# Two graph layers on one core: layer 1's constants and first load written beside layer 0, and the steps of a slot in another order

## The chip, the cores and the metric

The kernel runs on one core of one Trainium2 chip. The metric is device time in microseconds (us), as the median of several executions. The engines are TensorE (PE: matmuls; its weight loads, PEld, overlap them), VectorE (DVE), ScalarE (ACT), GpSimd (POOL) and SyncE (SP), which here only issues DMAs. Each engine takes its own instructions strictly in the order in which the program lists them, so an instruction that waits holds all that stands behind it on that engine.

## The reference

Sixteen graphs of 1024 nodes with 256 features go through two graph attention layers; each adds its result to its input and normalises the rows. Cut to what is computed:

```python
# layer 0: one head, dense softmax, three batch norms
Wh = einsum('bnf,of->bno', h, W);  ei = Wh @ a1;  ej = Wh @ a2
att = bn(ei[:, :, None] + ej[:, None, :], g1, b1)     # statistics over batch and rows
att = bn(where(att >= 0, att, 0.2 * att), g2, b2)
att = softmax(att, axis=2) * adj
x = layernorm(x + elu(bn(einsum('bij,bjo->bio', att, Wh), g3, b3)))

# layer 1: four heads, softmax over the neighbours only, mixed with softmax(adj)
fts = inputs @ Wh;  f1 = fts @ w1h + b1h;  f2 = fts @ w2h + b2h
logits = f1[:, :, None] + f2[:, None, :]
coefs = ah * softmax(leaky_relu(logits, 0.2) - 1e9 * (1 - adj)) + (1 - ah) * softmax(adj)
out = mean over heads of elu(coefs @ fts + bh + inputs)
x = layernorm(x + out)
```

The adjacency is sparse: a few neighbours in a thousand for most nodes, far more for the first ones.

## The kernel before

**Layer 0** (lines 200 to 645) is laid out by a scheduler that follows the dependencies and keeps each engine's list in an order near that of the code. It has three stages. *Projections* (lines 218 to 305): for each graph x is loaded (SP), transposed (PE), copied (ACT, L285), multiplied by WX (PE, L289) into one of four PSUM buffers `pw`, copied to `wx` (DVE, L293) and stored. The layer 1 weights W1s are loaded here too, and `WW` (the weights times w1 and w2) is made from them by DVE; `parameters1` loads bias, b1, b2 and alpha and waits for them on DVE. *Moments* (lines 318 to 512): statistics of the batch norms. *Aggregation* (lines 517 to 645): for each graph, weights (ACT, DVE), matmuls with `wh` (PE, L572), and a store to `h_dram` (SP, L599); `store` also collects sums, from which s3 and t3, scale and shift of the last batch norm, follow after the last graph.

**Between the layers.** Line 1023 makes t31. Then the pools of layer 1 open and lines 1035 to 1136 make its constants, nearly all on DVE: `IW` (identity and WW side by side), `MX` (mixes the heads), `bits`, `ibits`, `every`, `add16` (matmul weights that pack the bits of the adjacency into words), `cols`, `in8`, `in16`, `far`, `rows`, `low`, `act`, `lanes` (used to turn positions into lists of neighbours), the subtraction of W's last row `wl` from W1s, and the fixed parts of `fw` and `xr`. `wl` takes one of the two buffers that the rows of the adjacency (`rw`) and the lists' `B` use; `jj` one of those of `pi`. The pool `hpool` holds one buffer for a graph's h.

**Layer 1** (from line 1138) is written under `manual_schedule`: the order of the code is the order on each engine. For each graph g there is

- *Lists*: load_rows (SP, rw), words (PE: pc) and worded (ACT, DVE), used (DVE), places (PE: pp) and placed (DVE: hi, low), low and high (DVE: B, hA), higher (DVE), pick (PE: po, 64 matmuls) and picked (DVE), order (PE: pl) and indices (DVE: ix).
- *Graph*: load_h, exps (ACT) and elu (DVE), load_x, turn (PE: pz) and residual (DVE) and beside (ACT: fs) for eight blocks of rows, means, squares, spans, norm, factors, raised (ACT), scale (ACT, eight times 256 columns, L1481), table (SP: the scaled rows and their factors to `xe_dram`), spread, total (PE: pX) and store_total (SP: xr), gather_last and gathered (PE: pul, DVE: zl, ACT: sl), turn_last (PE: ptl).
- *Chunk*: fetch (POOL: an indirect DMA of neighbours' rows from `xe_dram` to xc) and weigh (DVE, one cast on ACT).
- *Unit*: sixteen per graph, two (hp 0 and 1) for each block of 128 rows: gather (PE: pu), invert (DVE: z), norm (ACT: s), turn (PE: pt) and turned (ACT: sT), linear (PE: pv), add (DVE: v), exps (ACT: m), sum, mean, squares, span, power (POOL), close (ACT), store (SP).

The PSUM pools are small: `ps_s` has two buffers, shared by pc, pz, pp, po, pl, pX, pA, pul and ptl; `ps_t` has one (pt), `ps_v` two (pv), `ps_u` three (pu).

The loop at line 1808 goes through slots n. In a slot, the unit n gathers, the unit n - 3 is turned, the unit n - 5 goes through linear, and so on, as the offsets in the code say. The side steps of the graphs (Lists, Graph, Chunk) stand in the slots that the tables `AT`, `FETCH` and `WEIGH` name, counted from the graph's first unit; a graph's steps begin 30 slots ahead of its first unit, so those of the next graph lie beside the units of this one, 16 slots apart. `side` sorts them into four lists for each slot: `early` (part 0: what reads a matmul's result, one slot after it), `first` (part 1: matmuls), `after` (part 2: DMAs and ACT), `late` (part 3: weigh). `gather(0)` has work only where hp is 0 (even slots: blocks 0 and 1), `gather(1)` in every slot. Slots of negative n, which have no units yet, are the lead of layer 1.

## Time and profile before

| | us |
|---|---|
| median of 3 runs | 2375.66 (2374.55 to 2377.97) |
| the profiled execution, as timed | 2380.35 |
| its span in the profile | 2378.5 |

| engine | busy us | share | instructions |
|---|---|---|---|
| PE | 2121.5 | 89% | 12631 |
| PEld | 1641.9 | 69% | 12631 |
| DVE | 1890.4 | 79% | 4624 |
| ACT | 1442.5 | 61% | 3172 |
| POOL | 1031.7 | 43% | 1133 |

How to read it. A group or timeline line names the engine, the line of the program (L1434), the operation, the tiles (what is written, an arrow, what is read) and the shapes; a number in brackets is the time for which the engine stood idle before it, and what ended that. The shares are averages over stages with different limits, so what a change is worth is read from its own stage: the moments keep DVE busy (80 of 115 us from 185 to 300), the aggregation PE, and in layer 1 both are busy most of the time. The granted clock of PE is 0.92 of full speed on average; it is low where PE's work is thin. A wait costs time only where the waiting engine, or one that waits for it, decides the end.

### The profile page before, as it was taken

To read this page: it belongs to the slowest core of one execution; us is meant where nothing else is said; L and a number is where in the kernel's file an instruction comes from. 1 tells how busy PE (TensorE), PEld (TensorE's weight loads), DVE (VectorE), ACT (ScalarE), POOL (GpSimd) and SP (SyncE) were. 2 spreads that over 40 slices of the span, in tenths; PEclk is the share of its full clock that TensorE was granted. 3 is DMA by queue.
4 is the path that set the end of the run, shared out by engine and by line. 5 is a ranking of instruction groups with operands and counts; after the bars stand their busy time and mean duration, and the time that the engine had idled before them with its cause. 6 is when DMAs were issued, how large, how long until landed. Compare 5 with 4: busy or idle time off the path is not lost. (4 is left out here: it accounts for less than half of the span.)

```text
span 2378.5 us, 37080 instructions
## 1 busy us (share of the span) xinstructions
PE 2121.5 (89%) x12631; PEld 1641.9 (69%) x12631; DVE 1890.4 (79%) x4624; ACT 1442.5 (61%) x3172; POOL 1031.7 (43%) x1133
## 2 busy tenths in 40 slices
PE   6992489999999549999999999999999999999997
PEld 5772434444444338878888788788888788887886
DVE  3335899999999446988888879888888889788786
ACT  1122777777776235567566665675776666757665
POOL 0000100000000037665766666756767666667682
PEclk9995589999999758999999999999999999999999
DMA  9969949986553258566575676675766756756551
GB/s 258 283 193 235 262 112 241 229 206 155 154 156 86 107 151 215 172 168 170 169 194 170 156 209 167 162 192 164 187 174 172 194 162 163 214 161 163 136 146 50
DMA packets 342358, 419.75 MB, mean 176 GB/s; under 512 B 172760, under 2 KB 273168, under 8 KB 336016
## 3 DMA queue, kind: packets, MB, share of 16 engines
q1 hardware_dynamic: 285840, 256.24, 36.7%
q0 software_dynamic: 55104, 158.54, 29.9%
q8 instruction: 102, 1.67, 0.3%
q10 hardware_dynamic: 1216, 2.51, 0.3%
q14 instruction: 96, 0.79, 0.1%
HBM read 346.47 MB, written 104.29 MB: 190 GB/s over the span
## 5 line engine op out<-in xcount | busy, mean ns | idle before, releaser
L1338 POOL DMA_INDIRECT xc<-xe_dram,ix x640 | 673.3, 1052 | 182.5 <-issue 162.0
L1635 PE MATMUL pv<-W1s,sT 128*128 128x256 f32 x2048 | 493.1, 384 | 0.3 <-ACT sT L1629 0.3
L572 PE MATMUL pa<-em,wh 128*128 128x512 f32 x1024 | 451.5, 599 | 18.0 <-DVE em L536 13.7
L1635 PEld LDWEIGHTS pv<-W1s,sT 128*128 128x128 f32 x2048 | 372.0, 192 | 40.9 <-ACT sT L1629 0.7
L572 PEld LDWEIGHTS pa<-em,wh 128*128 128x128 f32 x1024 | 193.6, 192 | 251.1 <-issue 236.4
L1543 PE MATMUL pu<-xc,w 128*125 128x256 f32 x1280 | 366.2, 408 | 0.0
L1615 PEld LDWEIGHTS pt<-MX,s 125*128 125x128 f32 x2560 | 338.2, 198 | 23.9 <-ACT sT L1625 6.3
L1615 PE MATMUL pt<-MX,s 125*128 125x100 f32 x2560 | 333.0, 279 | 4.4 <-ACT sT L1625 4.4
L1609 ACT ACTIVATE s<-pu,z 125x256 f32<-125x256 f32 x640 | 261.9, 477 | 21.6 <-DVE z L1601 21.4
L1543 PEld LDWEIGHTS pu<-xc,w 128*125 128x125 f32 x1280 | 243.5, 201 | 41.1 <-DVE v L1659 5.7
L1625 ACT COPY sT<-pt 128x500 f32<-128x500 f32 x256 | 148.5, 580 | 129.9 <-PE pt L1615 129.9
L1649 ACT ACTIVATE m<-v,neg 128x512 f32<-128x512 f32 x256 | 184.2, 719 | 49.9 <-DVE v L1643 37.0
L528 ACT ACTIVATE e<-eb,c,s 128x1024 f32<-128x1024 f32 x128 | 155.0, 1236 | 79.0 <-DVE sm L542 42.6
L1643 DVE TENSOR_TENSOR v<-pv,x 128x512 f32<-128x512 f32 x256 | 175.2, 684 | 12.4 <-PE pv L1635 12.0
L1451 ACT COPY fs<-pz 128x16 f32<-128x16 f32 x128 | 21.9, 171 | 250.9 <-DVE mv L1444 250.9
L532 ACT ACTIVATE e<-e,v,u 128x1024 f32<-128x1024 f32 x128 | 152.3, 1229 | 22.7 <-DVE e L531 16.6
L536 DVE TENSOR_TENSOR em<-e,mt 128x1024 f32<-128x1024 f32 x128 | 155.7, 1218 | 3.4 <-PE pa L572 2.1
L1434 PE MATMUL pz<-IW,h 128*128 128x136 f32 x512 | 94.0, 316 | 70.1 <-ACT fs L1451 27.1
L531 DVE SCALAR_TENSOR_TENSOR e<-e 128x1024 f32<-128x1024 f32 x128 | 151.5, 1217 | 0.0
L1434 PEld LDWEIGHTS pz<-IW,h 128*128 128x128 f32 x512 | 76.8, 208 | 90.6 <-ACT fs L1451 36.2
L147 POOL TENSOR_TENSOR s<-var,mhalf 128x2 f32<-128x2 f32 x1 | 0.7, 710 | 311.9 <-DVE var L146 311.9
L289 PE MATMUL pw<-WX,xT 128*128 128x266 f32 x512 | 124.5, 396 | 11.4 <-ACT xT L285 9.1
(319 smaller groups left out, 3602.2 us busy)
## 6 DMA issues: line engine op xcount, KB each, us to landing
x<-in_x_dram SPq DMA_DIRECT2D x32, 1024.0 KB
adj<-in_adj_dram POOLq DMA_DIRECT2D x16, 2048.0 KB, 16.7
rw<-adj SPq DMA_DIRECT2D x32, 1024.0 KB
A<-u_dram SPq DMA_DIRECT2D x128, 250.0 KB
wh_dram<-wx SPq DMA_DIRECT2D x16, 1024.0 KB
wh<-wh_dram SPq DMA_DIRECT2D x16, 1024.0 KB
h_dram<-hb SPq DMA_DIRECT2D x16, 1024.0 KB
h<-h_dram SPq DMA_DIRECT2D x16, 1024.0 KB
```

The costliest lines, as they stand in the source:

```text
L528: nc.scalar.activation(e, ebs[b], AF.Identity, bias=c1[:, k, b : b + 1], scale=s1[:, k : k + 1])
L532: nc.scalar.activation(e, e, AF.Exp, bias=v2[:, k : k + 1], scale=u2[:, k : k + 1])
L536: nc.vector.tensor_tensor(em, e, mts[b][:, k, :], ALU.mult)
L572: nc.tensor.matmul(acc[b, hf, oc], wh[b][:, k, oc * P : (oc + 1) * P], ems[b, k][:, hf * HALF : (hf + 1) * HALF], start=(k == 0), stop=(k ...
L1338: nc.gpsimd.indirect_dma_start(out=self.xc[:, i, :], out_offset=None, in_=xe_dram[g.b % 2], in_offset=bass.IndirectOffsetOnAxis(ap=g.l.ix[ ...
L1434: nc.tensor.matmul(pz[:, oc, :], self.h[:, oc, k * P : (k + 1) * P], IW[:, oc, :], start=True, stop=True,)
L1543: nc.tensor.matmul(pu[0:QR, 0:F], c.w[:, k].rearrange("p h q -> p (h q)"), c.xc[:, k, 0:F], start=(i == 0), stop=(i == len(OF[q]) - 1),)
L1609: nc.scalar.mul(f.s[0:QR, i], f.pu[i][0:QR, 0:F], f.z[0:QR, i : i + 1])
L1615: nc.tensor.matmul(self.pt[:, i].rearrange("p h q -> p (h q)"), self.first.s[0:QR, i, self.hp * P : (self.hp + 1) * P], MX[0:QR].rearrange ...
L1635: nc.tensor.matmul(self.pv[:, hh, :], self.first.sT[:, fc, self.hp * HP + hh, :], W1s[:, fc, self.hp * HP + hh, :], start=(fc == 0), stop= ...
L1643: nc.vector.tensor_tensor(self.v2, self.pv, self.g.x[:, self.it].unsqueeze(1).to_broadcast([P, HP, F]), ALU.add)
L1649: nc.scalar.activation(self.m, self.v2, AF.Exp, bias=neg1, scale=1.0)
```

## The change

The diff does three things.

1. The block that makes layer 1's constants moves, unchanged in what it computes, from between the layers to just behind the projections of layer 0. Its tiles get a pool of their own, `ek`, which is opened, together with `hpool`, ahead of layer 0 and closed at the end. `jj` and `wl` take the buffer of `hpool` (tag h) instead of those of `pi` and `rw`. In the list of the changed program the pieces lie on DVE among the copies of `wx` of the first five graphs, the iota on POOL at the very start, and `wl`'s DMA on SP behind the load of x of graph 9.
2. h of graph 0 is loaded to that buffer by a DMA written at n = 4 of the last graph of layer 0 (on SP it stands right behind the store of graph 0's h); `load_h` of graph 0 only takes it.
3. In layer 1 the order of the steps in a slot changes, and some entries of AT and FETCH move by one to three slots. On ACT, DVE and SP the steps of a slot keep their order relative to each other; on POOL, power stands at the head of the slot; on PE, gather(0) stands ahead of the side matmuls (`first`) instead of behind them.

```diff
+    m1 = ExitStack()
+    ek = m1.enter_context(tc.tile_pool(name="ek", bufs=1))
+    hpool = m1.enter_context(tc.tile_pool(name="hpool", bufs=1))

     with ExitStack() as l0:
...
             mts = {b: mask(mpool, b, "mt0") for b in range(min(2, B))}
+
+        TW = P + 2 * H
+        IW = ek.tile([P, C, TW], F32, name="IW")
+        for oc in range(C):
+            nc.vector.tensor_copy(IW[:, oc, 0:P], ident)
+        nc.vector.tensor_copy(IW[:, :, P:TW], WW)
...
+        jj = hpool.tile([P, K, NQ], I32, tag="h", name="jj")
+        nc.gpsimd.iota(jj, pattern=[[P, K], [0, NQ]], base=-N, channel_multiplier=1)
...
+        wl = hpool.tile([P, H, F], F32, tag="h", name="wl")
+        nc.sync.dma_start(wl, W[:, F - 1, :].partition_broadcast(P))
+        for fc in range(C):
+            nc.vector.tensor_tensor(W1s[:, fc], W1s[:, fc], wl, ALU.subtract)
+        nc.sync.dma_start(W1s[P - 1 : P, C - 1], bias1[0:1])
...
+        h0 = hpool.tile([P, C, N], F32, tag="h", name="h_0")

         epool = l0.enter_context(tc.tile_pool(name="epool", bufs=1))
...
+                    if n == 4 and b == B - 1:
+                        nc.sync.dma_start(h0, h_dram[0])
...
     with ExitStack() as l1:
         xpool = l1.enter_context(tc.tile_pool(name="x1pool", bufs=3))
-        hpool = l1.enter_context(tc.tile_pool(name="hpool", bufs=1))
         pk = l1.enter_context(tc.tile_pool(name="pk", bufs=1))
...
-        TW = P + 2 * H
-        IW = pk.tile([P, C, TW], F32, name="IW")
...
-        jj = pk.tile([P, K, NQ], I32, tag="pi", name="jj", bufs=1)
...
-        wl = pk.tile([P, H, F], F32, tag="rw", name="wl", bufs=2)
...
             def load_h(self):
                 b = self.b
+                if b == 0:
+                    self.h = h0
+                    return
...
         EARLY = 30
         AT = {
-            'lh': -29, ('rw', 0): -29, ('rw', 1): -28, ('words', 0): -24, ('words', 1):
-            -22, 'used': -20, 'places': -20, 'low': (-18, -18, -17, -15), 'high': (-19,
-            -15), 'higher': -14, 'pick': -14, 'order': -12, 'lx': -23, 'spans': -12,
-            'norm': -11, 'scale': (-11, -10), 'table': -9, 'spread': -10, 'total': -9,
+            'lh': -29, ('rw', 0): -29, ('rw', 1): -28, ('words', 0): -27, ('words', 1):
+            -22, 'used': -20, 'places': -20, 'low': (-18, -18, -17, -16), 'high': (-19,
+            -15), 'higher': -14, 'pick': -14, 'order': -11, 'lx': -23, 'spans': -12,
+            'norm': -11, 'scale': (-11, -11), 'table': -9, 'spread': -10, 'total': -9,
             'mean': (-17, -14), 'elu': (-26, -25, -24, -23), 'turn': (-22, -21, -19,
-            -19, -18, -17, -15, -15), 'gather': -4, 'turn last': -2,
+            -19, -18, -17, -15, -15), 'gather': -4, 'turn last': 0,
         }
 
         FETCH = {
-            'l': (-7,), 0: (-7, -7, -6, -6, -6), 'm': (-6, -6, -5, -5, -4), 'n': (-4,
-            -4), 1: (-4, -3, -3, -3, -2), 'o': (-2, -2), 2: (-1, -1, 0, 0, 0), 3: (1, 1,
-            1, 2, 2), 4: (2, 3, 3, 3, 3), 5: (3, 3, 4, 5, 5), 6: (5, 5, 6, 6, 7), 7: (7,
+            'l': (-7,), 0: (-7, -6, -6, -6, -6), 'm': (-6, -6, -5, -5, -4), 'n': (-4,
+            -4), 1: (-4, -3, -3, -3, -3), 'o': (-2, -2), 2: (-1, -1, 0, 0, 0), 3: (1, 1,
+            1, 1, 2), 4: (2, 3, 3, 3, 3), 5: (3, 4, 4, 4, 5), 6: (5, 5, 6, 6, 7), 7: (7,
             8, 8, 8, 10),
         }
...
             for n in range(-EARLY, len(units) + 12):
+                do(n - 9, "power")
                 do(n - 6, "add")
                 stand(0, n)
                 do(n - 6, "exps")
                 do(n - 3, "turn", "turned")
                 do(n - 1, "invert")
                 do(n - 1, "norm")
+                stand(2, n)
+                do(n - 10, "close")
+                do(n - 11, "store")
                 do(n - 5, "linear")
-                do(n - 9, "power")
-                stand(2, n)
+                if 0 <= n < len(units):
+                    units[n].gather(0)
                 stand(1, n)
-                do(n - 10, "close")
+                if 0 <= n < len(units):
+                    units[n].gather(1)
                 do(n - 7, "mean")
                 do(n - 8, "span")
                 stand(3, n)
-                do(n - 11, "store")
-                if 0 <= n < len(units):
-                    units[n].gather(0)
+                do(n - 6, "sum")
                 do(n - 7, "squares")
-                do(n - 6, "sum")
-                if 0 <= n < len(units):
-                    units[n].gather(1)
+    m1.close()
```

## The prediction

> **What bounds the kernel now.** I read the page first (span, busy shares, the 40 slices), then busy times by stage, then the waits of TensorE (PE), VectorE (DVE) and GpSimd (POOL) inside layer 1, then the timelines of the joint between the layers and of one graph.
>
> First two of the page's slices lines (busy tenths, 2378.5 us in 40), then the windows of three stages (length, busy us of PE, PE's weight loads, DVE, ACT, POOL, then granted clock, DMA share, GB/s): layer 0's aggregation, the joint, layer 1's loop.
>
> ```profile
> PE   6992489999999549999999999999999999999997
> DVE  3335899999999446988888879888888889788786
> ...
> 300.00:797.00 497.00, 488.17 (x1407) 237.67 (x1407) 455.73 (x534) 354.63 (x406) 8.11 (x12) 0.98 0.65 163
> 797.00:914.00 117.00, 56.63 (x407) 43.18 (x406) 65.77 (x278) 35.71 (x99) 38.61 (x37) 0.59 0.50 152
> 914.00:2357.00 1443.00, 1374.98 (x8969) 1193.23 (x8968) 1209.25 (x3340) 949.63 (x2529) 958.96 (x1032) 0.95 0.65 171
> ```
>
> Layer 0's aggregation is PE's (488 of 497 us). The joint, 797 to 914, is nobody's: PE works 57 of 117 us. Layer 1 looks like PE's (1375 of 1443), but the next two windows, of one graph, show two halves: 41 us in which PE never stops, then 46 us in which DVE is busy 44.83.
>
> ```profile
> 1662.00:1703.00 41.00, 41.00 (x299) 34.98 (x299) 31.38 (x83) 32.34 (x78) 25.24 (x28) 1.00 0.81 217
> 1703.00:1749.00 46.00, 42.74 (x254) 37.06 (x253) 44.83 (x134) 26.93 (x80) 34.38 (x37) 0.94 0.54 150
> ```
>
> PE's waits in layer 1 (in total, times, longest) all stand in that second half; DVE's long ones are for DMA, just ahead of it:
>
> ```profile
> PE pz L1434 <- ACT sl L1556: 23.3, 14, 1.7
> PE pz L1434 <- ACT fs L1451: 18.4, 12, 2.6
> PE pz L1434 <- DVE hi L1200: 13.8, 10, 2.3
> PE po L1259 <- ACT fs L1451: 6.1, 12, 0.5
> ```
>
> ```profile
> DVE mi L1353 <- DMA xc<-xe_dram,ix: 20.1, 8, 4.8
> DVE x L1444 <- DMA x<-in_x_dram: 17.2, 10, 2.8
> ```
>
> In the joint, the DVE timeline shows the constants ahead of the first ELU, and the first residual add waiting for x:
>
> ```profile
> 803.35 0.64 DVE L1038 COPY IW<-ident 128x128 f32<-128x128 f32 x2
> ...
> 812.63 1.27 DVE L1428 SCALAR_TENSOR_TENSOR h<-hm,h 128x512 f32<-128x512 f32 x2
> ...
> 822.85 0.42 DVE L1444 CUSTOM_DVE_ANT_0 x<-pz,x 128x256 f32<-128x256 f32 x1 [2.23 <-DMA x<-in_x_dram]
> ```
>
> And PE, in one graph (pz waits; matmuls after a wait; the pick group po):
>
> ```profile
> 1653.17 6.03 PE L1259 MATMUL po<-hA,B 128*128 128x64 f16 x64 [0.50 <-ACT fs L1451]
> ...
> 1716.04 0.76 PE L1434 MATMUL pz<-IW,h 128*128 128x136 f32 x4 [1.67 <-ACT sl L1556]
> 1716.61 1.90 PE L1543 MATMUL pu<-xc,w 128*125 128x256 f32 x4
> ...
> 1723.07 0.73 PE L1434 MATMUL pz<-IW,h 128*128 128x136 f32 x4 [0.93 <-ACT fs L1451]
> ```
>
> **The change, part by part.** Slots are numbered within a graph as in AT, so -14 is the slot of the pick, and -14 of one graph is 2 of the graph before it.
>
> *Constants, at the joint.* DVE has them from 803.35 to 812.63, 9.3 us. ScalarE (ACT), with two buffers hm, stops after two pairs of exp and scale: its third exp starts at 813.33 where it could at about 806.6, so the ELU gains 6.7 us. The second rows load (rw) is issued at 813.88, because it shares a buffer with wl; x queues behind it on SP (815.29) and lands at 822.85. Without wl all three loads go out from 803.8 in about 1.5 us of issue; 3.1 MB at the 283 GB/s of the page's busiest slice take 11 us, so x lands near 815. The chain behind (residual, words, places, pick, factors) starts 7.8 us earlier: -7.8.
> The next step in that chain is the table. Its DMAs leave at 857.21, when ACT has done four scales (851.61 to 853.58), an exp and scale of graph 1, and four more scales (855.13 to 857.09). With 'scale' (-11, -11) the eight stand together, which takes 1.55 us out from before the table: -1.6. POOL's first gather waits for that table (868.14). What is late next is the x of graph 1, which DVE awaits for 7.23 us at 870.5; it stands behind the same chain on SP and moves with it. Sum -9.4; bounds -12 (the 9.3 of the constants, the 1.6 and a little of graph 1's) and -4 (if x lands no earlier than 819.05, when the second rows load did).
> *Loading h of graph 0 in layer 0* is worth nothing: before, it already leaves SP at 770.45, ready for the 803.38 exp. In the new program's order it stands on SP right behind the store of h_0 (364.37) and holds the following eb, wh and mask loads until that store has landed. What covers it: the eb behind it feeds weights of the graph after the next, a whole period of 26 us (364.37 to 390.31) later. Cover gone, it would cost once at most the 5 us that a 1 MB load took at 813.88: 0.
>
> *Constants, in the projections.* The new program's order puts them between the copies of wx, where DVE has 0.46 us free per 0.90. Two of IW's copies stand ahead of WW, on the path to the first projection: 0.64 us. The two subtractions on W1s (2.36 us) follow wl's DMA, queued on SP behind x loads near 61 us; the like bias load took 11 us (42.35 to 53.3), so wl lands at about 72, and DVE reaches the subtraction at about 67. A stall of that kind is in the trace: DVE waits 4.84 us for al_bc and PE loses 2.39. The wx copies queue behind it, and PE waits for them once four pw buffers are full. I take 0.6 + 2.4 = +3; bounds 0 (wl early) and +6 (both ends of that stall, plus the subtractions).
>
> *Order of steps.* ACT, DVE and SP keep their sequence within a slot; power's place on POOL is the same relative to the gathers. What moves is on PE: gather(0), which has work in even slots only, now stands before the side steps. (a) Slot -18: two blocks, 0.87 us, stand ahead of the pz that waits for fs (12 times, 18.4 us; mostly 0.93 or 2.59): 0.87 covered. (b) Slot -14: four pairs, 1.7 us, go ahead of po, which covers its 0.50 and delays po by some 1.2 us less what (a) brought. Behind po PE runs at half rate for about 3.3 us whatever stands there (a pair takes 1.19 us instead of 0.59), so the slow stretch moves to the next turn and is not saved. DVE, which awaits po for 2.23 us, gets it 0.3 us later and has room in the PE half, where it is busy 31 of 41 us. So 0.87 x 12 + 0.50 x 12 = -16.4. The waits in slot -19 (sl, hi: 37 us) are in an odd slot, where nothing stands before them: they stay. Bounds: -24.5 (18.4 + 6.1, all of both) and +19 (if DVE decides behind po too, 15 graphs x 1.25).
>
> *Eight scales together.* Four more of 516 ns in slot -11 put ACT 2.06 us behind, with raised, exps and sT queued after them; ps_t has one buffer, so PE's turn two slots on waits for sT. Before: that sT copy ends at 1677.75, the turn starts at 1678.85. But words(0) (0.94 us) and order (0.22) move into the slots in between: 1.1 + 1.16 - 2.06 = 0.2 us left, cost 0. Bounds 0 and +31 (15 x 2.06). The gain is that the table leaves at about 1678.5 instead of 1682.13: xr, the gathers (POOL awaits xr 49.1 us in all) and the next x share the queues with less. These are DVE's waits of 20.1 + 3.4 + 17.2 = 40.7 us, ahead of the half in which DVE decides, so they count. x is issued no earlier and only lands faster; I take a quarter, -10, with bounds -41 and 0 (+8, a fifth of them, if the queues only swap places).
>
> *words(0) three slots earlier.* The rows loads leave at 1659.10 and the DMA share falls from 0.81 to 0.36 at 1670; words(0) would come at about 1674: covered by 3 us, else PE waits: 0. *low, order, turn last, FETCH:* same work, moved by one or two slots on engines that aren't waited for there; POOL issues every 1.26 us either way: 0, bounds -3 and +8 (20 per cent of the 40.7).
>
> **Sum.** -9.4 + 3 - 16.4 - 10 = -32.8. The profiled execution took 2380.35 us (span 2378.5 and 1.85 around it); it is 0.2% above the median of 2375.66. 2380.35 - 32.8 = 2347.5, in proportion 2343 of the median.
>
> **A rule weighed.** The 1.67 us wait at 1716.04 is followed by half rate: four gather matmuls take 1.90 us, where four took 1.03 at 1703.83, and ten turns 2.08 instead of 1.26, 1.7 us lost; the granted clock of the DVE half is 0.94. By these rows a removed wait could save up to 1.7 us more in each of 12 graphs, -20; as the waits of 0.93 in slot -18 are followed by full rate, I add nothing. The Trainium skill, "TensorE: Matmul & The Clock Gate", Part 1, has the clock halved only after an idle window of about 3.4 us. By the page, no wait of this loop is long enough to slow PE, and the sum would stay at -32.8 whatever happens to them; the trace disagrees.
>
> **Rivals.** (1) Only the joint gains: DVE decides throughout, what PE wins in -18 and -14 is awaited again at po, and the queues give nothing. For it: DVE's 44.83 of 46 us; against: PE never stops from 1755 on. -9.4 + 3 = -6, 2369. (2) The loads gain more: DVE's 40.7 us go almost wholly, hi shortens with them. For it: graphs with a late gather are those where hi is awaited (10 waits). -9.4 + 3 - 16.4 - 35 = -58, 2318. (3) Slower: ACT with eight scales in slot -11 is late for sT, PE stops 2.06 us in each of 15 graphs, and each stop brings the slow clock of 1716.61 with it (1.7 us): +56 against -33, so 2399. It decides from a stop of 2.2 us per graph, clock included, which is 0.5 us of stop; the margin was 0.2 us. (4) The constants stall the projections as much as they leave the joint (+6 against -4) and the slots give nothing: 2378.
>
> **How the numbers follow.** A difference of 0.2%, 4.8 us, is about what a measurement can tell. Forecast (2330 to 2357) 0.55; rival 1 (2360 to 2372) 0.18; rival 2 (below 2330) 0.12; rival 3 0.10; rival 4 0.05. Faster: 0.55 + 0.12 + 0.18 of rival 1, nearly all below 2371, 0.85; same: rival 4, 0.05; slower: rival 3, 0.10. The range of 8 in 10 leaves out the tails of 2 and 3: 2323 to 2371.
>
> **What would show it.** Right: the first ELU within 2 us of t3; x residual near 815 us after the span's start plus what the projections lost; no wait of pz for fs in slot -18 above 1.7; po after four gather pairs with no wait; table DMAs about 3.5 us earlier in the graph. Wrong: PE's turn waiting for sT copies 15 times; words waiting for rw; DVE waiting over 5 us for wl with PE losing more than 3; DVE busy through the PE half.

## The result, and the profile after

The changed kernel takes 2369.65 us in the median of 12 runs (2360.81 to 2377.86), the kernel before on the same chip 2375.11 (2366.84 to 2378.33): a ratio of 0.9976 with a 95% interval of 0.9959 to 0.9992. The profiled execution took 2365.66 us (span 2363.9) and is 4 us below its median, as the one of before was 5 us above its own; so sizes below are medians where they can be, and the profiles tell where. Beside the experiments, in another group of runs, the changed kernel ran again: 2354.67 against 2368.96, ratio 0.9936 (0.9918 to 0.9955). The change gains 5 to 14 us. The prediction, 2343, took it for 33.

The slices of the page after, then windows of the joint, of layer 1's loop, and of the two halves of one graph (length, busy us of PE, PE's weight loads, DVE, ACT, POOL, then granted clock, DMA share, GB/s):

```profile
PE   7893479999999759999999999999999999999997
DVE  4335899999999356888988978888889888798886
```

```profile
797.00:914.00 117.00, 67.34 (x463) 50.69 (x463) 60.79 (x183) 39.62 (x109) 41.24 (x39) 0.68 0.51 163
914.00:2357.00 1443.00, 1379.80 (x8959) 1200.23 (x8957) 1211.89 (x3357) 955.88 (x2534) 958.93 (x1033) 0.95 0.65 170
...
1654.00:1695.00 41.00, 41.00 (x301) 34.65 (x300) 32.07 (x90) 33.80 (x83) 29.57 (x32) 1.00 0.85 212
1695.00:1742.00 47.00, 42.90 (x264) 38.03 (x263) 42.34 (x122) 26.80 (x81) 33.71 (x35) 0.96 0.51 143
```

The joint holds 67 us of PE's work instead of 57: the first unit turn (the first pt of a unit, from where layer 1's loop is counted below) comes 8.06 us earlier (906.40 instead of 914.46). The loop looks as it did: a half in which PE never stops, and a half in which PE lacks 4 us. PE's and DVE's waits in layer 1 (in total, times, longest):

```profile
PE pz L1445 <- ACT sl L1567: 21.5, 14, 1.7
PE pz L1445 <- DVE hi L1208: 11.6, 10, 2.8
PE pz L1445 <- ACT fs L1462: 10.6, 7, 1.7
PE pt L1626 <- ACT sT L1636: 9.5, 21, 1.8
```

```profile
DVE wl L1179 <- ACT fw L1175: 57.9, 14, 5.1
DVE ptt L1277 <- PE po L1267: 51.9, 15, 4.2
DVE mi L1361 <- DMA xc<-xe_dram,ix: 15.7, 6, 4.3
```

The wait at po is gone and that for fs is shorter here (the section on why the prediction was wrong says what from), but turns wait for sT 21 times where they waited twice. DVE waits 52 us for po instead of 34; gather(0) now stands ahead of po on PE, which fits it. The 57.9 us for fw are words(0) of the next graph, which reach DVE before ACT is done with the eight scales.

PE in one graph after, the lines that answer to those of before (sl in slot -19, fs in -18, the turn of -17, po in -14):

```profile
1705.22 0.73 PE L1445 MATMUL pz<-IW,h 128*128 128x136 f32 x4 [1.67 <-ACT sl L1567]
...
1709.50 1.03 PE L1554 MATMUL pu<-xc,w 128*125 128x256 f32 x4
1712.25 0.73 PE L1445 MATMUL pz<-IW,h 128*128 128x136 f32 x4 [1.72 <-ACT fs L1462]
...
1713.69 1.94 PE L1626 MATMUL pt<-MX,s 125*128 125x100 f32 x10 [0.28 <-ACT sT L1636]
...
1736.45 6.04 PE L1267 MATMUL po<-hA,B 128*128 128x64 f16 x64
1742.33 1.20 PE L1554 MATMUL pu<-xc,w 128*125 128x256 f32 x2
```

The gather of 1709.50 does stand ahead of the side matmul, as the change wants it. The wait behind it is still 1.72 us long, and the turn after it runs at a lower rate (1.94 us, 1.25 in its neighbours). In the graph before, which waits longer for hi, the slow turn is the one of slot -18, and there is no wait for fs behind it:

```profile
1610.76 0.70 PE L1445 MATMUL pz<-IW,h 128*128 128x136 f32 x4 [1.67 <-DVE hi L1208]
1613.13 1.28 PE L1445 MATMUL pz<-IW,h 128*128 128x136 f32 x4 [1.67 <-ACT sl L1567]
1614.20 1.91 PE L1554 MATMUL pu<-xc,w 128*125 128x256 f32 x4
1615.90 2.30 PE L1626 MATMUL pt<-MX,s 125*128 125x100 f32 x10
1617.99 2.28 PE L1646 MATMUL pv<-W1s,sT 128*128 128x256 f32 x8
...
1620.97 0.62 PE L1445 MATMUL pz<-IW,h 128*128 128x136 f32 x4
```

The joint, on DVE, from t31 on:

```profile
807.54 0.17 DVE L1136 TENSOR_SCALAR t<-t 128x2 f32<-128x2 f32 x1
815.00 0.19 DVE L1179 TENSOR_REDUCE wl<-pc 128x8 f32<-128x32 f32 x1 [7.28 <-ACT fw L1175]
816.73 0.69 DVE L1439 SCALAR_TENSOR_TENSOR h<-hm,h 128x512 f32<-128x512 f32 x1 [1.54 <-ACT h L1432]
...
822.10 0.41 DVE L1455 CUSTOM_DVE_ANT_0 x<-pz,x 128x256 f32<-128x256 f32 x1
```

t31 comes 4.4 us later than before (803.17), and the constants are gone from behind it. Yet the first ELU stands 9.2 us after t31, as it did (9.5): now it is words(0) of graph 0, at -27, that stands ahead of it and waits for its rows. The first residual is 14.6 us after t31 instead of 19.7, and the table leaves after 47.3 instead of 54.0.

### The profile page after: what moved, and what is told of

Read it like the earlier page. It is cut to its first block, busy times and chain, and to the rows that moved or that the text cites. A ratio compares the mean times of both kernels' runs of the same rounds, so it can differ in the third digit from the quotient of the medians.

```text
span 2363.9 us, 37097 instructions
## 1 busy us (share of the span) xinstructions
PE 2129.9 (90%) x12631; PEld 1651.6 (70%) x12631; DVE 1883.8 (80%) x4624; ACT 1446.2 (61%) x3172; POOL 1032.6 (44%) x1133
## 3 DMA queue, kind: packets, MB, share of 16 engines
q8 instruction: 102, 1.67, 0.3%
## 5 line engine op out<-in xcount | busy, mean ns | idle before, releaser
L1646 PE MATMUL pv<-W1s,sT 128*128 128x256 f32 x2048 | 509.1, 393 | 0.3 <-ACT sT L1640 0.3
L683 PE MATMUL pa<-em,wh 128*128 128x512 f32 x1024 | 451.8, 599 | 17.9 <-issue 13.4
L1646 PEld LDWEIGHTS pv<-W1s,sT 128*128 128x128 f32 x2048 | 384.8, 198 | 45.3 <-ACT sT L1640 0.7
L1626 PEld LDWEIGHTS pt<-MX,s 125*128 125x128 f32 x2560 | 349.5, 205 | 39.2 <-ACT sT L1636 24.0
L1554 PE MATMUL pu<-xc,w 128*125 128x256 f32 x1280 | 360.0, 396 | 0.7 <-ACT s L1620 0.7
L1626 PE MATMUL pt<-MX,s 125*128 125x100 f32 x2560 | 350.8, 288 | 9.9 <-ACT sT L1636 9.5
L1554 PEld LDWEIGHTS pu<-xc,w 128*125 128x125 f32 x1280 | 235.2, 194 | 37.6 <-DVE omv L1675 5.7
L643 ACT ACTIVATE e<-e,v,u 128x1024 f32<-128x1024 f32 x128 | 152.3, 1229 | 22.7 <-DVE e L642 16.6
L1703 POOL TENSOR_TENSOR ors<-ors,mhalf 128x1 f32<-128x1 f32 x128 | 93.4, 730 | 165.4 <-DVE ors L1697 163.6
```

The source lines that it names most:

```text
L643: nc.scalar.activation(e, e, AF.Exp, bias=v2[:, k : k + 1], scale=u2[:, k : k + 1])
L683: nc.tensor.matmul(acc[b, hf, oc], wh[b][:, k, oc * P : (oc + 1) * P], ems[b, k][:, hf * HALF : (hf + 1) * HALF], start=(k == 0), stop=(k ...
L1554: nc.tensor.matmul(pu[0:QR, 0:F], c.w[:, k].rearrange("p h q -> p (h q)"), c.xc[:, k, 0:F], start=(i == 0), stop=(i == len(OF[q]) - 1),)
L1626: nc.tensor.matmul(self.pt[:, i].rearrange("p h q -> p (h q)"), self.first.s[0:QR, i, self.hp * P : (self.hp + 1) * P], MX[0:QR].rearrange ...
L1646: nc.tensor.matmul(self.pv[:, hh, :], self.first.sT[:, fc, self.hp * HP + hh, :], W1s[:, fc, self.hp * HP + hh, :], start=(fc == 0), stop= ...
```

## The experiments

All times are medians, of 4 to 12 runs; ratios are to the kernel before in the same group, with 95% intervals. The runs came in five groups, each on one chip. In two of them (called the stalling groups below, the kernel before at 2478 and 2473 us) layer 1 of every kernel took about 100 us more, with idle time on the engines that ended for nothing that the profile shows; the last section has the lines. What is concluded rests on the other three (2375.47, 2368.96 and 2370.09).

| kernel | ratio | interval | us |
|---|---|---|---|
| changed, first runs | 0.9976 | 0.9959 to 0.9992 | 2369.65 |
| changed, again | 0.9936 | 0.9918 to 0.9955 | 2354.67 |
| e1 joint alone | 0.9996 | 0.9982 to 1.0011 | 2374.53 |
| e2 slots alone | 0.9960 | 0.9946 to 0.9973 | 2366.62 |
| e7b joint and order, old tables | 0.9947 | 0.9932 to 0.9962 | 2358.03 |
| e3 wl loaded early | 0.9965 | 0.9952 to 0.9978 | 2367.88 |
| e4 words(0) back at -24 | 0.9994 | 0.9977 to 1.0011 | 2375.16 |
| e10 late parameters | 0.9919 | 0.9901 to 0.9937 | 2351.14 |
| e8b lists early | 1.0013 | 1.0003 to 1.0024 | 2372.22 |
| e9b no second half of high | 0.9932 | 0.9915 to 0.9950 | 2355.04 |
| e11 no first half of high | 1.0327 | 1.0314 to 1.0341 | 2446.39 |
| e12 lists later | 0.9847 | 0.9833 to 0.9861 | 2333.52 |
| e13 e10, lists and pick later | 0.9774 | 0.9760 to 0.9788 | 2315.81 |

**Parts of the change.** e1_joint_alone is the changed kernel with the old AT, FETCH and order of steps:

```diff
-            'lh': -29, ('rw', 0): -29, ('rw', 1): -28, ('words', 0): -27, ('words', 1):
+            'lh': -29, ('rw', 0): -29, ('rw', 1): -28, ('words', 0): -24, ('words', 1):
...
-                do(n - 9, "power")
                 do(n - 6, "add")
...
+                do(n - 9, "power")
```

> The constants and the load of h of graph 0 moved into layer 0, slots of layer 1 as before the change. Theory A (in layer 1 VectorE decides the half of a graph from slot -5 to the pick, so the new order and tables only shuffle waits, and the joint is all that gains): 5 to 9 us below the kernel before, that is about the whole of what the full change gave or a little more; from the first to the last unit turn 1443 us as before; the first ELU some 6 us earlier after t31, as the prediction had it, since words of graph 0 stands at -24 again. Theory B (order and tables do gain some 15 us or more, and the move of the constants loses it again): at or above the time before, 2375 to 2385.

e2_slots_alone is the kernel before with the new AT, FETCH and order:

> The new order of steps and the new AT and FETCH alone, the constants between the layers as before. Theory A: within 4 us of the kernel before (2371 to 2379), the layer 1 loop between first and last unit turn 1437 to 1447 us, PE's wait for fs shorter and its wait for sT longer by about the same. Theory B: 15 us or more below the kernel before (2360 or less).

e7_new_order and e7b_new_order (the same kernel twice) are the changed kernel with the old AT and FETCH; e6_old_order and e6b_old_order with the old order:

> The changed kernel with the old AT and FETCH; constants, h0 and order of steps as changed. Theory C: first unit turn 100 to 102 us after t31 (the order's share of the lead, without the table's 3 us), loop as before the change, 2371 to 2374. Rival (the order itself gains in the loop as the prediction had it, 16 us, and the tables give it back): 2358 or below.

> The same kernel as e7_new_order (old AT and FETCH, new order), for a chip without the stalls. Theory C: first unit turn 100 to 102 us after t31, loop within 4 us of the kernel before, in all 4 to 8 us below it. Rival (the order gains 16 us in the loop, the tables give it back): 15 us or more below it.

> The changed kernel with the old order of steps in a slot; constants, h0, AT and FETCH as changed. Theory C (of the lead's 12.4 us between t31 and the first unit turn about 7 come from the constants' move, about 3 from the table that leaves before the exps of graph 1, and the rest from gather(0) standing ahead of the side matmuls; the loop gains nothing from any of it): first unit turn 101 to 102 us after t31, loop as in the changed kernel, time 2 to 4 us above it, 2371 to 2373. Rival (the order is what the tables need, or the tables what the order needs): the loop longer by 5 us or more, 2376 or above.

> The same kernel as e6_old_order (constants, h0, AT and FETCH as changed, old order), for a chip without the stalls. If the order is what gains (the runs with the new order and the old tables stood at 0.9947, with the old ones of both at 0.9996): 2 to 5 us below the kernel before, that is the joint and the table's 3 us of the lead, ratio 0.998 to 1. If the tables gain as much by themselves: 0.995 or below.

Measured: the joint alone gains nothing that can be told, 0.9996; the slots alone 0.9960; joint and order 0.9947. Theory A had it the other way round, and theory B's 15 us or more from the slots were 9. Joint and order gained 12 us, between theory C's 4 to 8 and its rival's 15. In the profile of e1 the joint does what it should, DVE from t31 (805.74) on:

```profile
807.64 0.69 DVE L1439 SCALAR_TENSOR_TENSOR h<-hm,h 128x512 f32<-128x512 f32 x1 [1.73 <-ACT h L1432]
...
818.42 0.42 DVE L1455 CUSTOM_DVE_ANT_0 x<-pz,x 128x256 f32<-128x256 f32 x1 [2.43 <-DMA x<-in_x_dram]
```

The first ELU is 1.9 us after t31, the first residual 12.7 (7.0 less than before), the first unit turn 104.6 instead of 111.3: 6.7 us won. But t31 itself is later: 806.1 on average over the fourteen profiles with the constants in the projections (804.1 to 809.0), 802.1 over the two without (801.05 and 803.17). What is left, 2.7 us, is 0.11%, inside the interval of e1 (0.9982 to 1.0011).

The slots by themselves give 7.0 us in the lead: in e2 the first unit turn is 104.3 us after t31. The table leaves 2.1 us earlier there, though the first residual is where it was; in e7b, with the old table, the order alone has 102.0 against 104.6 in e1. With both, 98.9 in the changed kernel. From the first unit turn to the end (the median less that turn's time) the kernel before has 1461 us, e2 1461, the changed kernel 1463 and, run again, 1446, where the kernel before (its turn taken at 914.5) would have 1454; e1 has 1464 and e7b 1451 (the kernel before there: 1456). So order and tables are worth between +2 and -8 us inside the loop. Single profiles don't settle it better: from the first unit turn to the last, the kernel before has 1442.9 us, e1, with the same layer 1, 1436.4, e2 1439.1, e7b 1431.9, and the changed kernel 1436.3 and 1424.9, so the same steps differ by 6.5 and 11.4 us. The order can be the whole of the gain: e7b has it without the tables. The fourth combination, tables without the order, only ran in stalling groups (e6: 1.0024, 1.0002 to 1.0047; e6b: 1.0066, 1.0034 to 1.0098; e7 there 0.9982, 0.9950 to 1.0014), so what the tables do without the order stays open.

**What the constants cost in the projections.** In the changed kernel DVE stands 4.04 us for al_bc and, some 16 us later, for wl:

```profile
56.41 0.17 DVE L196 TENSOR_SCALAR om_bc<-al_bc 128x4 f32<-128x4 f32 x1 [4.04 <-DMA al_bc<-in_L_gnn_alpha_dram]
...
72.30 1.23 DVE L400 TENSOR_TENSOR W1s<-W1s,wl 128x1024 f32<-128x1024 f32 x1 [7.35 <-DMA wl<-in_L_gnn_W_dram]
```

e3_wl_early loads wl behind the first six x:

```diff
             for b in range(min(6, B)):
                 load_x(b)
+            wl = apool.tile([P, H, F], F32, name="wl")
+            nc.sync.dma_start(wl, W[:, F - 1, :].partition_broadcast(P))
```

> The changed kernel, but wl is loaded right behind the first six x, ahead of the first wh store, so that VectorE does not stand 7.35 us for it and PE 4.51. Theory A (that stall is what the constants cost in the projections, 4.4 us up to the last aggregate of layer 0, and nothing absorbs it): no wait for wl, last aggregate of layer 0 near 797 us instead of 801.4, the time 3 to 5 us below the changed kernel, 2365. Rival (the projections wait for x loads anyway, or the transfer ahead of wh delays them): the wait goes to another tile, no change within 2 us.

Measured: no wait for wl, and t31 at 807.28, as late as ever. The rival's first half is right, the wait goes to other tiles. DVE in e3:

```profile
58.04 0.69 DVE L192 TENSOR_SCALAR bias<-bias 128x1024 f32<-128x1024 f32 x1 [6.01 <-DMA bias<-in_L_gnn_bias_dram]
...
63.38 0.17 DVE L196 TENSOR_SCALAR om_bc<-al_bc 128x4 f32<-128x4 f32 x1 [3.97 <-DMA al_bc<-in_L_gnn_alpha_dram]
```

Loading early did not help here, where the DMA engines are 0.9 busy (from 20 to 110 us): with one more transfer ahead, the next ones came late. e10_late_params leaves the parameters' loads among those of the first graphs, puts that of wl with them, and moves what waits for them:

```diff
-        nc.vector.tensor_scalar(bias1, bias1, 1.0, None, ALU.add)
-        nc.vector.tensor_scalar(om_bc, al_bc, -1.0, 1.0, ALU.mult, ALU.add)
...
+                if b == 8:
+                    late(nc.vector.tensor_scalar(bias1, bias1, 1.0, None, ALU.add))
+                    late(nc.vector.tensor_scalar(om_bc, al_bc, -1.0, 1.0, ALU.mult, ALU.add))
+                    late(nc.vector.tensor_copy(al2, al_bc))
+                    for fc in range(C):
+                        late(nc.vector.tensor_tensor(W1s[:, fc], W1s[:, fc], wl, ALU.subtract))
```

> The changed kernel with layer 1's parameters (bias, b1, b2, alpha) and wl loaded where they were, but what VectorE makes of them (bias + 1, 1 - alpha, the two subtractions of wl, MX) placed behind the copies of graph 8. Theory D (the projections lose to whichever load VectorE meets too early: wl 7.35 and al_bc 4.04 us in the changed kernel, bias 6.0 and al_bc 4.0 where wl was loaded first; transfers take over 10 us there with the DMA engines 0.9 busy): no wait of VectorE over 1 us in the projections, last aggregate of layer 0 at 795 to 796 us, 6 us before the changed kernel's 801 to 802, and the whole time 4 to 7 us below it. Rival (the projections are bound by the x loads, the stalls only use their slack): last aggregate near 801, no gain.

Measured: DVE waits for no load any more in the projections, and t31 comes at 799.33 (796.98 and 801.27 in the two later kernels with the same layer 0): 7 us before the changed kernel's average, and 2.9 before that of the kernel before, which has the stall for al_bc as well. So theory D holds for layer 0, and the rival (bound by the x loads) falls. The whole time is 3.5 us below the changed kernel of the same group, under the 4 to 7 expected, with intervals that overlap.

**words(0) and the eight scales.** e4_words_back puts one entry back:

```diff
-            'lh': -29, ('rw', 0): -29, ('rw', 1): -28, ('words', 0): -27, ('words', 1):
+            'lh': -29, ('rw', 0): -29, ('rw', 1): -28, ('words', 0): -24, ('words', 1):
```

> The changed kernel with words(0) at -24 again and nothing else. Theory A (words(0) at -27 puts its cast and its reduction, which wait for the rows load, ahead of the first ELU, and that is why the ELU did not get the 6.7 us): the first ELU 6 us earlier after t31, first unit turn 0 to 5 us earlier; VectorE's 57.9 us of waits for fw go back to about 12, without gain in the loop as they lie in PE's half; the time 0 to 5 us below the changed kernel. Rival (early words are what keeps the loop from losing, as PE would wait for them): the loop between first and last unit turn longer by 5 us or more.

Measured: the first ELU is at 1.89 us after t31, the residual at 12.8. The first unit turn does not get it (99.7, in the changed kernel 98.9): the table leaves 2.1 us earlier, and the first fetch follows at 57.3 us instead of 56.9. And the median is 7.3 us above that of e3, which differs from the changed kernel only by the place of wl's load and of what reads it, and had t31 as late. PE's waits in e4 have more for sT (in e3 12.8 us, 23 times):

```profile
PE pt L1626 <- ACT sT L1636: 20.3, 45, 2.5
```

Without words(0) in slot -11, nothing stands between the eight scales and the turn of slot -10, which waits for sT; that slot takes 4.9 us on average instead of 4.3. But slot -19 takes 7.2 instead of 7.7, and in the two profiles the loop from the first unit turn to the last is as long, 1440.6 us and 1439.6 in e3. So the longer wait is shown, and that it makes the 7.3 us of the medians is not: by the rival's own measure, a loop longer by 5 us or more, the rival falls.

**Does VectorE decide the half?** The prediction's second half of a graph had DVE busy 44.83 of 46 us. Two kernels change DVE's work there. e9 leaves out four instructions of 0.44 us in slot -15 (the lists then miss neighbours in the rows 64 to 127 of a block), e8 moves list steps into PE's half:

```diff
             def high(self, part):
-                if part == 0:
-                    self.A = pk.tile([P, 8, K, NQ], FP16, tag="hA", name=f"hA_{self.b}", bufs=1)
+                self.A = hA
+                if part == 1:
+                    return
```

```diff
-            -22, 'used': -20, 'places': -20, 'low': (-18, -18, -17, -16), 'high': (-19,
-            -15), 'higher': -14, 'pick': -14, 'order': -11, 'lx': -23, 'spans': -12,
+            -24, 'used': -23, 'places': -22, 'low': (-21, -20, -19, -18), 'high': (-20,
+            -18), 'higher': -16, 'pick': -14, 'order': -11, 'lx': -23, 'spans': -12,
```

> The changed kernel without the second half of high (four instructions of 0.44 us in slot -15 of each graph; neighbours in the rows 64 to 127 of a block are left out of the lists, the transfers and matmuls stay the same in number and size). Theory A (VectorE decides slots -20 to -15): the whole 1.74 us comes out of each of 15 graphs and one more time in the lead, 24 to 28 us below the changed kernel, some 2343. Rival (TensorE and its clock decide): VectorE only waits longer for po, 2365 to 2371.

> The changed kernel with list steps moved earlier, words(1) -24, used -23, places -22, low -21 to -18, high -20 and -18, higher -16: 3.9 us of VectorE work per graph (used 1.05, placed 1.92, one low 0.95) leave the slots -20 to -14, in which VectorE is busy 98 per cent, for slots -23 to -21, where it has 2.3 us free beside TensorE. Theory A (VectorE's work decides slots -20 to -15): 2.5 us less in each of 15 graphs, 30 to 40 us below the changed kernel, some 2335. Rival (TensorE or its clock decides there as well): no gain, 2365 to 2373; or more where hi and pz waits return in the other half.

> The changed kernel itself, beside the next three on one chip. On a chip like that of the first runs 2366 to 2372, ratio to the kernel before 0.996 to 0.998; on a chip like that of the last four, where all four kernels and the kernel before took 100 us more in layer 1 and TensorE idled 45 to 68 us for nothing that the profile shows, some 2475.

> The same kernel as e9_no_high1, for a chip without those stalls. Theory A: 1.74 us in each of 15 graphs, 24 to 28 us below the changed kernel on the same chip. Rival: VectorE only waits longer for po, within 4 us of it.

> The same kernel as e8_lists_early, for a chip without those stalls. Theory A (VectorE's work decides slots -20 to -15): 30 to 40 us below the changed kernel on the same chip. Rival (TensorE or its clock decides): within 5 us of it.

In a stalling group e9 was 1.0099 (1.0065 to 1.0132) and e8 1.0001 (0.9972 to 1.0029). In the other, beside the changed kernel, 1.74 us less of DVE's work in each graph moved the time by 0.4 us (2355.04 and 2354.67), and lists early made it 17.6 us slower, which neither theory had. Theory A falls. About half of the time taken out of slot -15 comes back on DVE, in e9b, as a longer wait for po (53.1 us in the changed kernel of that group):

```profile
DVE ptt L1281 <- PE po L1271: 65.3, 14, 6.2
```

Cut finer, the half of the changed kernel is three stretches: slots -19 to -17, slots -16 to -14, and po.

```profile
1698.00:1718.00 20.00, 15.90 (x88) 13.35 (x86) 19.59 (x53) 9.74 (x29) 14.76 (x15) 0.91 0.50 129
1718.00:1738.00 20.00, 20.00 (x123) 18.21 (x122) 19.48 (x59) 14.00 (x43) 14.08 (x16) 1.00 0.52 159
1738.00:1743.00 5.00, 5.00 (x54) 4.91 (x53) 0.85 (x2) 2.42 (x8) 2.48 (x3) 0.86 0.49 124
```

DVE is as busy in the second as in the first, 19.5 of 20 us. But PE is idle 4.1 us in the first and never in the second, and in the third DVE waits 4.15 us. By this reading DVE decides in the first stretch alone; in the second it is only just fast enough. e8b put its steps on the wrong side: slot -20, ahead of the first stretch, became 6.8 us long instead of 5.56, and DVE is busy for 6.6 of them.

So work has to go from the first stretch to later ones. e12_lists_later moves 2.7 us of it and leaves nothing out, e11 leaves out the half of high that stands in slot -19 (neighbours in the rows 0 to 63). The edit of e12:

```diff
-            -22, 'used': -20, 'places': -20, 'low': (-18, -18, -17, -16), 'high': (-19,
+            -22, 'used': -20, 'places': -20, 'low': (-18, -17, -16, -15), 'high': (-16,
```

> The changed kernel with low at -18, -17, -16, -15 and high at -16 and -15: 2.7 us of VectorE work go from slots -19 and -18 to -17 to -15, nothing is left out. Theory E: TensorE's wait for sl goes and that for fs shrinks; VectorE has only 2.4 us between its last list step and the first matmul of po, so the gain is bounded by that, 10 to 35 us below the changed kernel. Rival: the same wait returns at po, within 5 us of it.

> The changed kernel without the first half of high (four instructions, 1.72 us, in slot -19; neighbours in the rows 0 to 63 of a block are left out of the lists, transfers and matmuls stay the same in number and size). Theory E (VectorE decides only slots -20 to -17: there TensorE waits for hi 1.6, sl 1.7 and fs 1.7 us and then runs at half rate; from slot -16 on TensorE is never idle, which is why leaving out the other half in slot -15 gave nothing): 1.7 us and some of the half rate in each of 15 graphs, 25 to 45 us below the changed kernel. Rival (TensorE's waits only move on to the next narrow place, the whole graph is paced by TensorE's work and its clock): within 5 us of the changed kernel, as without the other half.

Measured: e12 has 2333.52, ratio 0.9847. The changed kernel did not run beside it; against its ratios in the other groups, 0.9936 and 0.9976, that is 21 or 31 us less, in the range of theory E (10 to 35), and its nearest neighbour in the same group, e7b, is 24.5 us above it. The wait for sl is gone (14 waits, 21.5 us), and that for fs is at most 0.9. The windows of one graph of e12 and its PE lines:

```profile
1594.00:1614.00 20.00, 18.84 (x118) 16.20 (x117) 19.45 (x54) 10.92 (x33) 16.26 (x18) 1.00 0.53 125
1614.00:1631.00 17.00, 15.77 (x91) 13.62 (x90) 16.61 (x54) 8.59 (x26) 12.05 (x13) 1.00 0.50 137
```

```profile
1605.47 0.73 PE L1445 MATMUL pz<-IW,h 128*128 128x136 f32 x4 [0.56 <-ACT fs L1462]
...
1606.91 1.36 PE L1626 MATMUL pt<-MX,s 125*128 125x100 f32 x10 [0.28 <-ACT sT L1636]
...
1630.30 6.04 PE L1267 MATMUL po<-hA,B 128*128 128x64 f16 x64 [1.10 <-ACT fs L1462]
```

PE's idle time in the first stretch falls from 4.1 to 1.2 us, the granted clock there goes from 0.91 to 1.00, and 1.10 us of the gain is awaited again at po, 15.0 us in all. e11 can't be read as it was meant: it took 2446.39 us, not less, and its transfers were slower (last section); DVE waits 70.2 us there for A.

e13_pick_later is e10 with the same lists moved further, and the pick, with higher, one slot later:

```diff
-            'lh': -29, ('rw', 0): -29, ('rw', 1): -28, ('words', 0): -27, ('words', 1):
-            -22, 'used': -20, 'places': -20, 'low': (-18, -18, -17, -16), 'high': (-19,
-            -15), 'higher': -14, 'pick': -14, 'order': -11, 'lx': -23, 'spans': -12,
+            'lh': -29, ('rw', 0): -28, ('rw', 1): -27, ('words', 0): -25, ('words', 1):
+            -22, 'used': -20, 'places': -20, 'low': (-18, -17, -16, -15), 'high': (-16,
+            -14), 'higher': -13, 'pick': -13, 'order': -11, 'lx': -23, 'spans': -12,
```

> The kernel with the late parameters, and in layer 1 the pick one slot later (-13, with higher; low at -18 to -15, high at -16 and -14; rw at -28 and -27, words(0) at -25). Theory E: as with lists later, and VectorE's 3.9 us of waiting for po take list work too: 30 to 70 us below the kernel with the late parameters, less up to 9 us as words(0) no longer stands between the eight scales and the turn of slot -10. Rival: within 5 us of that kernel, or slower by those 9.

Measured: 2315.81, ratio 0.9774, the best of all: 54 us below the kernel before, and by the ratios some 34 below e10. Its waits of PE in layer 1, all but one of 0.3 us:

```profile
PE pt L1630 <- ACT sT L1640: 21.4, 59, 1.2
PE pz L1449 <- ACT fs L1466: 8.1, 12, 1.0
PE pz L1449 <- DVE hi L1212: 1.1, 4, 0.4
```

Of the 18 us that it is below e12, about 10 are the projections (t31 at 796.98 instead of 807.34) and 11 the lead (first unit turn 88.6 us after t31 instead of 99.6). What the later pick gives in the loop is not settled: from the first unit turn to the end the medians leave 1430 us, in e12 1427, but inside the profiles the loop from the first unit turn to the last is 1398.4, in e12 1412.0, and PE's waits in layer 1 are 30.9 us, in e12 44.7. The wait for po is gone, and the wait for sT is back, 59 times, since words(0) is no longer in slot -11. e14_pick_later_split tried to take that away with scale at -11 and -10:

> The kernel with the pick one slot later, and scale at -11 and -10 as before the change. With words(0) at -25 nothing stands between the eight scales and the turn of slot -10, and TensorE waits there 58 times for sT, 20 us in all. Theory F (that wait costs its length): the wait for sT goes to 2 us and the time is 5 to 15 us below the kernel with the pick later (2316, ratio 0.977), less what a table 3.5 us later costs. Rival (the table's place decides, or the clock): within 4 us of it.

It ran in a stalling group, 2455.51 against 2472.57, ratio 0.9940 (0.9909 to 0.9970), and cannot be set beside e13.

## Why the prediction was wrong

**The step that failed** is the sum of the order of steps, "So 0.87 x 12 + 0.50 x 12 = -16.4", and with it "I take a quarter, -10" for the queues. Together they forecast -26.4 us for the loop, which moved by +2 to -8. They rest on opposite readings of the same half: -16.4 takes PE's waits as time that PE's own work can cover, which holds where PE decides; -10 takes DVE's waits as time that counts, which holds where DVE decides.

- (a) "0.87 covered" in slot -18. In that slot it came about: where its turn runs at full rate (1.25 us), the wait for fs behind it was 2.59 us before and is 1.72 in the changed kernel, 0.87 less, and where the turn is slow (1.3 us or more) the wait was 0.9 to 1.2 us or none and is now 0.2 at most. (The totals, 18.4 us before and 10.6, 19.3, 19.0, 17.3 and 21.8 in changed, changed again, e2, e3 and e7b, hide it: they go by how many graphs are of each kind.) But the two slots behind take it back. The mean lengths in us of some of PE's slots, counted from turn to turn, in 14 graphs of each profile:

| | -19 | -18 | -17 | -16 | -18 to -16 |
|---|---|---|---|---|---|
| before | 8.52 | 7.37 | 4.28 | 6.63 | 18.3 |
| e1, layer 1 as before | 8.63 | 7.12 | 4.31 | 6.66 | 18.1 |
| changed | 8.11 | 6.45 | 5.01 | 7.09 | 18.6 |
| changed, again | 6.75 | 6.77 | 5.27 | 7.02 | 19.1 |
| e2, slots alone | 7.75 | 6.84 | 5.22 | 7.06 | 19.1 |
| e7b, old tables | 8.30 | 6.77 | 5.02 | 6.66 | 18.4 |
| e12, lists later | 5.97 | 5.94 | 4.72 | 7.21 | 17.9 |

  In slot -17 most turns now wait 0.28 us for sT or are slow (in e7b PE waits there for fs a second time, 0.6 us), and with the new tables the turn of slot -16 waits too, in about half of the graphs. Over the three slots nothing is gained, where 0.87 us in each of 12 graphs was forecast.

  What sets their length is DVE. The buffer that PE waits for is free when ACT has copied fs, and ACT waits for DVE's residual (below), which DVE reaches when it is through with the list work of slots -19 and -18. PE's own work put ahead of that wait does not bring its end nearer. e12 shows the other side: with DVE's work moved the waits for sl go, those for fs shrink, slots -19 to -17 fall from 20.2 us before to 16.6, and the time by 21 us or more. What the changed kernel's loop does gain lies in slot -19 (0.4 and 1.8 us a graph), where the prediction had the waits stay; its two profiles differ there by 1.4 us, so how much of that is the change's is open.
- (b) The 0.50 at po is covered, as forecast (6.1 us to nothing), and the half rate behind po moved to the next turn: 1.20 us for a pair at 1742.33, and in every graph the turn of slot -13 is slow (2.29 us). "It is not saved" was right. Slots -14 and -13 together are 17.2 us before, 17.0 in e1 and 16.7 to 17.1 in the profiles with the new order (changed, changed again, e2, e3, e7b, e10), so some 0.2 of the 0.50 was won on average; DVE's wait for po grew from 33.6 to 51.9 us.
- The queues. DVE's waits for the chunks and x, with the idle time ahead of the same instructions that the profile ascribes to nothing, did shrink by about what was taken: 41.0, 41.5 and 40.1 us without the new tables (before, e1, e7b), 34.9, 24.2, 35.1, 37.0 and 34.2 with them (changed, changed again, e2, e3, e10), 33 on average. But the time does not follow: e7b, without the tables, stands at 0.9947 beside 0.9976 and 0.9936 with them. In e7b turns wait 1.7 us for sT, in those five 9.5 to 12.8; that these 8 to 11 us of PE's are what the 8 us of DVE's were paid with fits the sizes, and was not tried by itself.

The lines for (a): in a graph of before, the turn of slot -18 at full rate and the wait for fs behind it (the one after is at 1712.25 above), then ACT's longest wait in layer 1 of the changed kernel (as run again):

```profile
1248.01 1.25 PE L1615 MATMUL pt<-MX,s 125*128 125x100 f32 x10
...
1253.61 0.73 PE L1434 MATMUL pz<-IW,h 128*128 128x136 f32 x4 [2.59 <-ACT fs L1451]
```

```profile
ACT fs L1462 <- DVE mv L1455: 187.5, 112, 4.0
```

**What held.** The constants at the joint: 7.8 us expected, 7.0 at the residual and 6.7 at the first unit turn where the joint stands alone. The table ahead of the exps: 1.6 expected; it leaves 6.75 us earlier where the residual is 5.1 earlier, so 1.65. Taken together the lead gains 12.4 us; the order's part of it, 2.6 in e7b, was not in the sum. The constants in the projections: +3 expected, +4.0 measured on the averages, by the stall that the prediction named; but its lower bound, "0 (wl early)", was wrong, since e3 is as late; in the changed kernel DVE waits 7.35 us for wl and PE loses 4.5, one of the prediction's own signs of being wrong. The eight scales: costed at nothing because words(0) and order stand in between; with both in place sT is awaited over 20 times, some 0.5 us each, which the prediction named as a sign of being wrong and did not have in its sum. e4 took words(0) away and the wait grew by 7.5 us, inside the 0 to 31. words(0): the ELU of graph 0 did not come earlier because of it, which the prediction missed, but nothing that follows waited for that. The load of h of graph 0 was not tried alone; in the profile after it is issued at 372.11 and the load behind it leaves at 372.53.

**The rule weighed.** The prediction set rows (1.67 us of waiting, then half rate) against the Trainium skill, "TensorE: Matmul & The Clock Gate", Part 1. (One wait in the loop of before is as long as the page's window, 3.4 us for sT; the waits in question are shorter.) In the loop of the changed kernel no wait of PE is longer than 2.8 us, and in 11 of 14 graphs a turn of slots -18 or -17 takes over 1.5 us for its ten matmuls. In e13, with no wait over 1.2 us, none does; in e12 two of 14 do, behind waits for hi of 4.21 and 1.65 us, and the twelve others, all but one with no wait over 1.1 us in these slots, run at full rate there. So a slow PE goes with waits below the page's 3.4 us here. "Only" was the prediction's word: the same Part 1 also has, under "A second HAM failure mode", a kernel in which frequent short idle times bring the clock down and up again. A slow slot -18 costs less than the 1.7 us that the prediction weighed: the slow rows of 1613.13 to 1617.99 take 2.8 us more than their neighbours, and have no wait of 1.7 us behind them, so about 1 us a graph is left. That may be part of what e12 gained; it was not tried by itself.

**The rivals.** Rival 1 has the measured number, 2369, and not the mechanism: it had the joint gain and the slots give nothing, and the runs show the joint near zero, since the projections take back what it wins, and the slots at 0.9960 alone. "DVE decides throughout" fell with e9b. Rival 2's waits did not go: 33 of DVE's 41 us are left. Rival 3's stop is real and was covered in part, as e4's wait for sT shows. Rival 4's stall is real too, and smaller than the joint's gain.

## What to carry to other kernels

An engine that is busy 97% of a stretch need not decide it: look for where the other engine waits inside that stretch, and cut the windows until one of the two is never idle. Terms of one sum should agree on who decides a stretch: a wait of PE covered and a wait of DVE shortened there do not both count. Work put ahead of a wait is worth something only if whoever ends the wait is not itself behind; here 2.7 us of list work moved out of the 20 us in which PE waited gained more than the whole change, and the same kind of work moved to the wrong side of them lost 18 us. The stall for a small load in a stretch with busy queues was mended here by moving the instruction that waits, not the load.

## What the runs showed that was not expected

*Half rate after short waits.* Three waits of 0.4 to 1.7 us within 10 us stand in a 20 us window with a granted clock of 0.91 and a turn of 1.94 instead of 1.25 us; the window of e12 above, with one wait of 0.56 and two of 0.3 us, has 1.00.

*Gathers from few places.* With the first half of high left out, the lists point to one row of zeros in the places of those neighbours. From 1000 to 2200 us the indirect DMAs (the first line of the queues) moved slightly less, and kept the DMA engines busy half as long again. The changed kernel, then e11 (packets, MB, share of 16 engines):

```profile
q0 software_dynamic: 30864, 100.45, 36.1%
```

```profile
q0 software_dynamic: 29340, 95.51, 54.8%
```

In e9b, with the other half left out, the share was 37.3%. That it is the one row that makes them slow was not tried.

*Groups that stand still.* In the two stalling groups layer 0 took its usual time (t31 at 801.3 to 807.7), and layer 1 some 100 us more. PE's waits there, e6 in such a group, hold a kind that no profile of the other groups has for PE, idle time that ended for nothing shown ("issue"):

```profile
PE pz L1445 <- ACT fs L1462: 34.5, 14, 2.6
PE pz L1445 <- issue: 31.3, 28, 2.1
```

Counted from 925 to 2345 us, with waits that the profile puts down to "remote" without naming an instruction, the six profiles of those groups have 45 to 68 us of it on PE and 61 to 124 on ACT; the others none on PE and at most 2 on ACT. The cause stays open, and so does whether it lies in the chip: the first stalling group and the group run after it, which does not stall, both ran on a chip numbered 0. For a comparison it means that a kernel is to be set beside the kernel before in the same group only, and that even the ratio of a stalling group says little.

*The same code at different times.* t31, at the end of the same layer 0, differed by 4.8 us between fourteen profiles (804.1 to 809.0), and whole runs of one kernel in one group mostly by 8 to 20 us outside the stalling groups. A term of 3 us in a sum like this one is only to be seen in profiles, and in several of them, not in the time.
